# Gate of the dense experts by one ScalarE silu in place of a sigmoid and a GpSimd product

## The chip, the cores and the metric

The kernel runs on one core of a Trainium2 chip as one launch. The metric is the device time of that launch in microseconds (us). The core has these engines: TensorE (PE in the profile; its weight loads are PEld), VectorE (DVE), ScalarE (ACT), GpSimd (POOL) and SyncE (SP). Each engine carries out its own instructions in order, and semaphores hold an instruction until what it reads is written.

## The reference, cut to what matters

The whole program is a chain of eight pairs of layers on 4096 tokens of 128 features. The change lies in the sixth pair, in its first layer (named L2_attn_b in the reference, "window" in the kernel), which is an attention followed by experts of its own; it touches the experts. Every token goes through all eight experts, hence "dense"; the routing weights of four of them are not zero.

```python
def moe(x, router_W, router_b, gup, gup_b, down, down_b):
    logits = flat.astype(jnp.float32) @ router_W + router_b
    w, idx = jax.lax.top_k(logits, TOP_K)                    # TOP_K = 4 of 8
    w = jax.nn.softmax(w, axis=-1) / TOP_K
    scores = jnp.zeros((T, N_EXPERTS), w.dtype).at[jnp.arange(T)[:, None], idx].add(w)
    gate_up = jnp.einsum('th,ehm->etm', flat, gup) + gup_b[:, None, :]
    gate = jnp.clip(gate_up[..., :INTER], NEG, LIMIT)        # LIMIT = 7, INTER = 128
    up = jnp.clip(gate_up[..., INTER:], -LIMIT, LIMIT)
    glu = gate * jax.nn.sigmoid(gate * ALPHA)                # ALPHA = 1.702
    gated = (up + 1.0) * glu
    eout = jnp.einsum('etm,emh->eth', gated, down) + down_b[:, None, :]
    out = jnp.einsum('eth,te->th', eout, scores)
```

With silu(z) = z * sigmoid(z), the gate is `glu = silu(1.702 * gate) / 1.702`. Since `gated` is multiplied by the token's routing weight for the expert, the factor 1/1.702 can be put into that weight.

## The kernel before, in words

Tokens lie along the free axis: a chunk is 128 features by 512 tokens, and there are eight chunks (`NCH` = 8, `CH` = 512). `window_moe` runs 64 units of work, unit i being expert i mod 8 of chunk i div 8. `tiles_in_slots` writes the order out by hand: slot k calls each step whose turn it is, later steps of the pipeline first, and within `manual_schedule` the engines get their instructions in that order. In slot k these are `narrow(k - 4)`, `gate(k - 2)` and `wide(k)`, then, every fourth or eighth slot, the steps of routing for the following chunk, and last the steps of the next stage's norm for chunks that are done (`late`, five chunks). All instructions are recorded by helpers, so the profile gives the helpers' lines: L504 matmul, L508 transpose, L528 ACT, L531 DVE tensor by tensor, L534 POOL tensor by tensor, L538 and L540 DVE tensor by scalar, L543 DVE scalar_tensor_tensor.

- `wide(i)`: two matrix products into two PSUM banks (two PE matmuls each in the trace). DVE reads the first as `g` (bias, minimum with 7, L540), ACT takes the sigmoid of 1.702 g into `sg` (L528), DVE reads the second as `u` (bias and 1, minimum with 8, L540), and POOL multiplies `g` by `sg` into `g` (L534).
- `gate(i)`: DVE computes max(u, -6) * g (L543, `u<-u,g`); POOL multiplies by the spread routing weight `rb` (L534, `u<-u,rb`).
- `narrow(i)`: the down product (`ps<-u,w`), summed over the eight experts of a chunk in one bank. The first expert's slot starts the sum with the product of routing weights and bias (`ps<-rt,w`). POOL adds the attention's residual to `x` at the fifth expert, and DVE adds the sum to `x` at the eighth (`x<-x,ps`).
- Routing: `compare` (logits on PE; `lg`, `equal`, `ahead`, `m` on DVE, two small products on POOL, exp on ACT), `choose` (DVE: `rank`, `lg`, `m`, `wide`), `turn` (PE transposes, ACT copies to `rt`) and `shares` (PE spreads four experts' weights over 128 partitions into four banks, ACT copies them to `rb`).

PSUM is shared as three banks `ps` for `wide`, four `r` for routing, spreads and norm, and one `o` for the sum. Of `g` there are four buffers, of `u` six, of `sg` three. Exp and Ln need another ACT table than sigmoid: `logs` loads the first, and the table for sigmoid is loaded ahead of the next sigmoid by the compiler. The chunk whose sum is complete is normalised for the next stage by `ha<-ps` (ACT), `nsq` (POOL), `nrs` (Ln and Exp on ACT) and `ha<-ha,nrs` (DVE). That next stage is `mix`; four small POOL products of its weights (`Wr`, `Wk`) are placed near the end of this one.

Of the kernel before, what the change touches and what calls it, by code (L numbers as in the profile page):

```python
# [11 lines left out]
F32, BF16, I32 = mybir.dt.float32, mybir.dt.bfloat16, mybir.dt.int32  # L12
SP = mybir.EngineType.SP
AF = mybir.ActivationFunctionType
ALU = mybir.AluOpType
AX = mybir.AxisListType

P = 128
B, T, C = 16, 256, 128
NT = B * T  # L20
CH = 512
# [470 lines left out]
class Net:  # L492
# [910 lines left out]
    def window_moe(self, w, h, n1):  # L1403
        x = self.x
        with ExitStack() as st:
            p1 = self.pool(st, "e1", 1)
            rt = p1.tile([8, NT], F32, tag="rt", name="rt")
            self.route(n1, w["gate"], 4, 0.25, rt, w["gate_b"])
            p2 = self.pool(st, "e2", 2)

            ub = p1.tile([P, 16], F32, tag="ub", name="ub")
            self.ts(ub, w["gub"], 1.0, ALU.add)
            for c in range(NCH):
                s = self.chunk(c)
                po = self.bank()
                self.mm(po, w["downb"], rt[:, s], stop=False)
                for e in range(8):
                    pg, pu, pb = self.bank(), self.bank(), self.bank()
                    self.mm(pg, w["gu"][:, e * 256 : e * 256 + P], n1[:, s])
                    self.mm(pu, w["gu"][:, e * 256 + P : e * 256 + 256], n1[:, s])  # L1420
                    self.mm(pb, self.sel[:, e, :], rt[:, s])
                    g = p2.tile([P, CH], F32, tag="g", name="g")
                    u = p2.tile([P, CH], F32, tag="u", name="u")
                    sg = p2.tile([P, CH], F32, tag="sg", name="sg")
                    self.ts(g, pg, w["gub"][:, 2 * e : 2 * e + 1], ALU.add, 7.0, ALU.min)
                    self.act(sg, g, AF.Sigmoid, scale=1.702)
                    self.stt(sg, g, -1e9, sg, ALU.max, ALU.mult)
                    self.ts(u, pu, ub[:, 2 * e + 1 : 2 * e + 2], ALU.add, 8.0, ALU.min)
                    self.stt(u, u, -6.0, sg, ALU.max, ALU.mult)
                    self.tt(u, u, pb, ALU.mult)  # L1430
                    self.mm(po, w["down"][:, e * C : e * C + C], u, start=False, stop=e == 7)
                self.tt(g, h[:, s], po, ALU.add)
                self.gt(x[:, s], x[:, s], g, ALU.add)
# [216 lines left out]
class Fast(Net):  # L1650
# [896 lines left out]
    def window_moe(self, w, h, n1):  # L2547

        x, nc = self.x, self.nc
        with ExitStack() as st:  # L2550
            p = self.stage(st, "e2", 1)
            compare, choose, turn = self.route_steps(st, w["gate"], 4, 0.25, w["gate_b"], "r")

            ub = p.tile([P, 16], F32, tag="ub", name="ub")
            self.ts(ub, w["gub"], 1.0, ALU.add)
            rts, rbs, gs, us, pos = {}, {}, {}, {}, {}

            def compared(c):
                self.logs(False)
                compare(c, n1)  # L2560

            def turned(c):
                rts[c] = turn(c)

            def shares(i):
                c, half = divmod(i, 2)
                rb = p.tile([P, 4, CH], F32, tag="rb", name="rb", bufs=2)
                for r, pb in enumerate(self.four(rts[c], self.k["sel4" + "ab"[half]], "r")):
                    self.act(rb[:, r], pb, AF.Copy)
                rbs[i] = rb  # L2570

            def wide(i):
                c, e = divmod(i, 8)
                s = self.chunk(c)
                pg, pu = self.bank(), self.bank()
                self.mm(pg, w["gu"][:, e * 256 : e * 256 + P], n1[:, s])
                self.mm(pu, w["gu"][:, e * 256 + P : e * 256 + 256], n1[:, s])
                g = p.tile([P, CH], F32, tag="g", name="g", bufs=4)
                u = p.tile([P, CH], F32, tag="u", name="u", bufs=6)
                sg = p.tile([P, CH], F32, tag="sg", name="sg", bufs=3)  # L2580
                self.ts(g, pg, w["gub"][:, 2 * e : 2 * e + 1], ALU.add, 7.0, ALU.min)
                self.act(sg, g, AF.Sigmoid, scale=1.702)
                self.ts(u, pu, ub[:, 2 * e + 1 : 2 * e + 2], ALU.add, 8.0, ALU.min)

                self.gt(g, g, sg, ALU.mult)
                gs[i], us[i] = g, u

            def gate(i):
                c, e = divmod(i, 8)
                self.stt(us[i], us[i], -6.0, gs.pop(i), ALU.max, ALU.mult)  # L2590
                self.gt(us[i], us[i], rbs[i // 4][:, e % 4], ALU.mult)

            def narrow(i):
                c, e = divmod(i, 8)
                if e == 0:
                    pos[c] = self.bank("o")
                    self.mm(pos[c], w["downb"], rts[c][:8], stop=False)
                self.mm(pos[c], w["down"][:, e * C : e * C + C], us.pop(i), start=False, stop=e == 7)
                s = self.chunk(c)
                if e == 4:  # L2600
                    self.gt(x[:, s], x[:, s], h[:, s], ALU.add)
                if e == 7:
                    self.tt(x[:, s], x[:, s], pos.pop(c), ALU.add)

            with self.share(ps=3, r=4, o=1):
                many = 8 * NCH
                late = [(8 * i + at, 8, NCH - 3, f) for i, at, f in zip((1, 2, 2), (4, 1, 2), self.lead(p, "r", tables=True))]
                self.tiles_in_slots(-7, many + 4, [
                    (4, 1, many, narrow), (2, 1, many, gate), (0, 1, many, wide),
                    (-1, 4, 2 * NCH, shares), (-3, 8, NCH, turned), (-5, 8, NCH, choose), (-7, 8, NCH, compared),  # L2610
                    *late,
                ])
# [1236 lines left out]
```

## Time and profile before

| what | value |
| --- | --- |
| time of the kernel, median of three runs | 4268.84 us (4268.18 to 4270.52) |
| time of the profiled execution | 4291.23 us |
| its span, first to last instruction | 4289.4 us |
| mean granted TensorE clock over the span | 0.949 |
| PE busy in the span | 3886.8 us (91%) |
| DVE busy | 2597.7 us (61%) |
| ACT busy | 2325.8 us (54%) |
| POOL busy | 1949.6 us (45%) |
| first product of `wide`, last of `narrow` in `window_moe` | 3418.0 us, 3652.4 us after the span's start |

The times in the trace come from one profiled execution. A group of the profile is a line, an engine, an operation and what it writes and reads, with its count, its busy time and mean duration, and the idle time of its engine just before it with what ended it. The timeline shows instructions in order of their start; a bracket at the end of a line holds the idle time before it and the instruction that ended it. Matmuls are pipelined and their ends are modelled, so the busy share of PE also holds time in which it waits.

### The profile page before, as it was taken

The numbers are of one execution on the slowest core, as the hardware profiler recorded it, in microseconds if no ns is written. First come the engines' busy times: TensorE is split into PE (matmuls) and PEld (weight loads), VectorE is DVE, ScalarE is ACT, GpSimd is POOL, SyncE is SP. The second block draws the span as 40 slices with busy tenths as digits, with TensorE's granted clock in tenths as the row PEclk, the third lists the DMA queues.
The fourth block names the chain that finished last, engine by engine and source line by source line (L and its number), as shares of the span: only waits on it lengthen the run. The fifth ranks groups of instructions, "written<-read, shape, count | busy, mean of one in ns | idle before, by whom it ended". The sixth has DMA issues, their size and how long they took to land. (4 is left out here: it accounts for less than half of the span.)

```text
span 4289.4 us, 73913 instructions
## 1 busy us (share of the span) xinstructions
PE 3886.8 (91%) x28998; PEld 2214.8 (52%) x28998; DVE 2597.7 (61%) x4503; ACT 2325.8 (54%) x4741; POOL 1949.6 (45%) x1696
## 2 busy tenths in 40 slices
PE   7999999998899999984989979888999999899978
PEld 3555466465465456553965549643444343455333
DVE  4775576374577377464336633555777698386474
ACT  6665466554766466552446634444555544674432
POOL 4664365232565166315433434454555498411251
PEclk8999999988999999997999979999999999999989
DMA  1800000000000000002930039100000000000000
GB/s 60 340 1 1 11 1 2 19 1 1 20 1 2 3 1 2 1 3 96 324 112 12 17 128 319 63 19 16 1 1 1 3 1 1 15 2 18 6 0 21
DMA packets 78404, 176.43 MB, mean 41 GB/s; under 512 B 12606, under 2 KB 39108, under 8 KB 77920
## 3 DMA queue, kind: packets, MB, share of 16 engines
q1 hardware_dynamic: 65568, 148.40, 10.0%
q0 software_dynamic: 9120, 18.51, 1.2%
q8 instruction: 231, 3.78, 0.4%
q10 hardware_dynamic: 3360, 4.72, 0.3%
q14 instruction: 125, 1.02, 0.1%
HBM read 118.28 MB, written 54.20 MB: 40 GB/s over the span
## 5 line engine op out<-in xcount | busy, mean ns | idle before, releaser
L528 ACT ACTIVATE pt<-ps 128x512 f32<-128x512 f32 x640 | 339.7, 600 | 325.1 <-PE ps L504 323.7
L504 PE MATMUL ps<-hb,w 128*128 128x512 f32 (+1 forms) x960 | 466.3, 619 | 8.8 <-issue 3.3
L504 PE MATMUL ps<-w,hb 128*128 128x512 f32 (+2 forms) x896 | 406.7, 575 | 25.4 <-DVE t L531 19.5
L534 POOL TENSOR_TENSOR t<-t,t 128x512 f32<-128x512 f32 x256 | 319.3, 1269 | 161.5 <-DVE t L531 101.5
L531 DVE TENSOR_TENSOR t<-ps,tab 128x512 f32<-128x512 f32 x512 | 317.6, 681 | 85.3 <-ACT sq L528 81.8
L534 POOL TENSOR_TENSOR t<-t,ss 128x1024 f32<-128x1024 f32 x128 | 243.5, 1903 | 218.7 <-ACT ss L528 217.5
L504 PEld LDWEIGHTS ps<-hb,w 128*128 128x128 f32 (+1 forms) x960 | 179.6, 192 | 270.5 <-issue 223.6
L528 ACT ACTIVATE qkt<-ps 128x512 f32<-128x512 f32 x256 | 140.5, 595 | 309.9 <-PE ps L508 309.3
L531 DVE TENSOR_TENSOR u<-u,ps 128x384 f32<-128x384 f32 (+1 forms) x206 | 121.8, 595 | 282.9 <-PE ps L504 122.4
L531 DVE TENSOR_TENSOR ot<-ps,rd 128x512 f32<-128x512 f32 (+2 forms) x224 | 143.3, 640 | 231.8 <-ACT rd L528 231.8
L534 POOL TENSOR_TENSOR nsq<-ha 128x512 f32<-128x512 f32 x112 | 123.1, 1099 | 322.0 <-ACT ha L528 305.0
L504 PEld LDWEIGHTS ps<-w,hb 128*128 128x128 f32 x896 | 156.8, 194 | 185.1 <-issue 115.4
L534 POOL TENSOR_TENSOR both<-pt 128x1024 f32<-128x1024 f32 x64 | 151.2, 2362 | 199.9 <-DVE pt L531 164.3
L504 PE MATMUL ps<-nsq,ct 128*128 128x512 f32 x368 | 203.6, 636 | 32.5 <-POOL nsq L534 27.6
L504 PE MATMUL ps<-ot,w 128*128 128x512 f32 x448 | 214.4, 613 | 17.3 <-DVE ot L531 9.2
L504 PE MATMUL ps<-u,w 128*128 128x512 f32 (+1 forms) x448 | 218.4, 611 | 8.4 <-POOL u L534 8.4
L2199 POOL DMA_INDIRECT back<-y,x x142 | 138.9, 978 | 185.5 <-ACT y L528 84.2
L504 PE MATMUL ps<-xt,w 128*128 128x128 f32 x1704 | 219.9, 279 | 1.7 <-ACT xt L528 1.5
L528 ACT ACTIVATE u<-ps,w 128x512 f32<-128x512 f32 x160 | 107.7, 685 | 183.1 <-PE ps L504 180.5
L504 PEld LDWEIGHTS ps<-xt,w 128*128 128x128 f32 x1704 | 203.7, 193 | 3.0 <-ACT xt L528 2.6
L3746 POOL DMA_INDIRECT rows<-out,idx x128 | 126.2, 986 | 170.2 <-ACT out L528 121.1
L528 ACT ACTIVATE nrs<-ps,ct 128x512 f32<-128x512 f32 x208 | 139.6, 683 | 103.2 <-PE ps L504 93.8
(363 smaller groups left out, 9095.3 us busy)
## 6 DMA issues: line engine op xcount, KB each, us to landing
w<-in_moe_x SPq DMA_DIRECT2D x142, 533.0 KB
rows<-t SPq DMA_DIRECT2D x64, 520.0 KB
x<-rows SPq DMA_DIRECT2D x142, 65.0 KB
w<-in_local_f SPq DMA_DIRECT2D x8, 659.5 KB
y<-back ACTq DMA_DIRECT2D x16, 256.0 KB
y<-back SPq DMA_DIRECT2D x16, 256.0 KB
w<-in_local_f SPq DMA_DIRECT2D x4, 658.5 KB
back<-y,x POOLq DMA_INDIRECT x142
```

Source lines behind the costliest of these rows:

```text
L504: self.nc.tensor.matmul(out, lhsT, rhs, start=start, stop=stop)
L528: self.nc.scalar.activation(out, in_, func, **kw)
L531: self.nc.vector.tensor_tensor(out, a, b, op)
L534: self.nc.gpsimd.tensor_tensor(out, a, b, op)
L2199: nc.gpsimd.indirect_dma_start(views[i], bass.IndirectOffsetOnAxis(ap=x[:, C : C + 1].bitcast(I32), axis=0), y, None, bounds_check=2 * NT ...
L3746: nc.gpsimd.indirect_dma_start(views[(c * 2 + k) * 4 + t], bass.IndirectOffsetOnAxis(ap=idx[:, k, t : t + 1], axis=0), out[:, k, t], None,)
```

## The change

In `window_moe`, ACT computes silu(1.702 g) and writes it over `g`; the sigmoid, its tile `sg` and the POOL product of `g` and `sg` are gone. The ACT copies of the spread routing weights from PSUM to `rb` multiply by 1/1.702.

```diff
                 for r, pb in enumerate(self.four(rts[c], self.k["sel4" + "ab"[half]], "r")):
-                    self.act(rb[:, r], pb, AF.Copy)
+                    self.act(rb[:, r], pb, AF.Copy, scale=1.0 / 1.702)
                 rbs[i] = rb
...
                 u = p.tile([P, CH], F32, tag="u", name="u", bufs=6)
-                sg = p.tile([P, CH], F32, tag="sg", name="sg", bufs=3)
                 self.ts(g, pg, w["gub"][:, 2 * e : 2 * e + 1], ALU.add, 7.0, ALU.min)
-                self.act(sg, g, AF.Sigmoid, scale=1.702)
+                self.act(g, g, AF.Silu, scale=1.702)
                 self.ts(u, pu, ub[:, 2 * e + 1 : 2 * e + 2], ALU.add, 8.0, ALU.min)
-
-                self.gt(g, g, sg, ALU.mult)
                 gs[i], us[i] = g, u
```

## The prediction

> **What bounds it now.** I read first the windows view, one row for each chunk of eight experts (from the start of a second expert's first matmul to the next chunk's; the last row runs to the final expert's down product). Columns: stretch, length, then busy us (instructions) of PE, PEld, DVE, ACT, POOL, granted clock, DMA.
>
> ```profile
> 3474.28:3504.39 30.11, 29.20 (x83) 12.48 (x82) 26.65 (x38) 15.42 (x24) 27.16 (x21) 0.94 0.00 1
> 3504.39:3533.16 28.77, 27.77 (x84) 11.75 (x82) 26.39 (x38) 15.29 (x24) 25.60 (x21) 1.00 0.00 1
> 3533.16:3564.85 31.69, 30.92 (x84) 12.88 (x82) 26.08 (x38) 15.53 (x24) 27.57 (x22) 0.89 0.00 0
> 3622.90:3652.44 29.54, 23.30 (x58) 9.42 (x57) 23.06 (x25) 7.64 (x12) 28.84 (x23) 0.90 0.00 1
> ```
>
> PE, DVE and POOL are all near full; ACT is half idle. Chunks at full clock take 28.8 us, those with a clock under 1 take 29.3 to 31.7. The groups of 3450 to 3630 and the tile views (min/median/max ns) say what fills DVE and POOL:
>
> ```profile
> L534 POOL TENSOR_TENSOR g<-g,sg 128x512 f32<-128x512 f32 x50 | 75.2, 1504 | 10.9 <-ACT sg L528 10.6
> L534 POOL TENSOR_TENSOR u<-u,rb 128x512 f32<-128x512 f32 x50 | 67.5, 1350 | 6.6 <-DVE u L543 6.6
> L531 DVE TENSOR_TENSOR ahead<-lg 128x256 f32<-128x256 f32 x6 | 8.9, 1485 | 0.0
> L531 DVE TENSOR_TENSOR lg<-lg,m 128x32 f32<-128x32 f32 x6 | 5.7, 954 | 0.2
> ...
> L543 DVE SCALAR_TENSOR_TENSOR u<-u,g x64: 678/1168/1742, 3426.4 to 3647.7; 128x512 f32<-128x512 f32 x64
> ```
>
> The g product is the larger half of POOL. The DVE product takes 678 ns at best and 1168 at the median, and `lg<-lg,m`, 32 columns wide, takes 954. They are long where a POOL product runs beside them. Then the timeline at a chunk boundary (start, us, instruction, idle before and its releaser):
>
> ```profile
> 3537.09 1.49 DVE L531 TENSOR_TENSOR ahead<-lg 128x256 f32<-128x256 f32 x1
> ...
> 3538.70 1.04 DVE L531 TENSOR_TENSOR lg<-lg,m 128x32 f32<-128x32 f32 x1
> ...
> 3539.78 0.23 ACT L528 ACTIVATE lg<-lg 128x32 f32<-128x32 f32 x1 [2.56 <-DVE lg L531]
> ...
> 3542.70 0.69 DVE L531 TENSOR_TENSOR ha<-ha,nrs 128x512 f32<-128x512 f32 x1 [0.45 <-ACT nrs L528]
> ...
> 3544.05 1.97 PE L504 MATMUL ps<-rt,w 8*128 8x512 f32 x2 [0.20 <-DVE x L531]
> ```
>
> Slow routing steps on DVE delay ACT's exp, this delays the norm's Ln and Exp, `ha` and `x<-x,ps` on DVE follow, and PE waits for the last before the new chunk's bias product, as there is one bank for the sum. Half speed follows: the trace's clock records show it at 3486.2 to 3489.6, 3544.2 to 3551.0 and 3605.6 to 3609.0. Last, the tail:
>
> ```profile
> 3647.66 1.74 DVE L543 SCALAR_TENSOR_TENSOR u<-u,g 128x512 f32<-128x512 f32 x1 [2.69 <-POOL g L534]
> 3648.81 2.93 POOL L534 TENSOR_TENSOR u<-u,rb 128x512 f32<-128x512 f32 x2
> 3650.57 3.38 PE L504 MATMUL ps<-u,w 128*128 128x512 f32 x4 [4.96 <-POOL u L534]
> ```
>
> PE ends on POOL's backlog: 12.0 us lie between the last expert's first matmul (3640.46) and its down product (3652.44).
>
> **What the Trainium skill says.** "GPSIMD Engine Reference", Specifications: GpSimd's SBUF interfaces are VectorE's too, with contention for DVE instructions that have two SBUF inputs. The trace agrees: 678 ns against up to 1742 for the same product, while the PSUM-fed `g<-ps,w` stays within 737 to 752. "ScalarE: Activation LUTs", Step-by-step: one element per cycle and lane whatever the function; What ACT_TABLE_LOAD costs: about 1283 ns for any set. The trace agrees: loads take 1283, and the silu of the sparse experts (`u<-ps`, 384 columns) takes 490 ns where a copy of 512 takes 579 to 597. "TensorE: Matmul & The Clock Gate", Part 1: a gate halves the clock after a window of low activity. The trace agrees on the half (a 128x512 matmul starts every 0.43 us, in those stretches every 0.85); what triggers it no view shows.
>
> **The change, part by part.** As built, PE, DVE, ACT and SP issue the same instructions in the same order in both kernels, table loads included; POOL issues 64 products fewer. No DMA or queue moves.
>
> *ACT.* 64 sigmoids become 64 silus of the same size in the same places: nothing, covered by ACT's 13.5 idle us in each 28.8. Their exact price is unseen, as no silu from SBUF of 512 columns is in the trace: from 0.60 us (the 490 and 0.83 ns a column for 128 more) to 0.70; I take sigmoid's 0.63. The scale in 64 copies is a constant in an instruction that is there already: 0, at most the 0.1 us between a copy's fastest and slowest, hidden as well. Writing `g` in place takes away the wait for one of three `sg` buffers (1.9 us once). `g` is held, as before, until DVE's product has read it.
>
> *POOL.* Out go 64 products of 1513 ns mean in the stage, 96.8 us. The stage keeps 116 us over about 230, so POOL stops being a bound. DVE's product waits for ACT instead of POOL; behind it on DVE are the next expert's two PSUM reads, and PE waits for those, as three banks serve two per expert.
>
> *DVE.* What contends is left with half its rival. The uncontended prices: product 0.68; `equal` 0.43 and `ahead` 0.41 (their minima), `lg<-lg,m` 0.19 to 0.51, `lg<-rank,lg` 0.19 and `m` 0.17 (the first chunk, whose routing ran while POOL was idle) against 0.87 and 0.73 now. The remaining POOL product starts when DVE's own ends, and the next two DVE instructions read PSUM, so these two kinds now miss each other.
>
> *PE, steady chunks.* From the fifth expert's start (3431.77) to the 58th's (3622.90) are 191.1 us. What PE must issue there, at its full pitch: 53 slots of six matmuls at 0.429, 136.4; 13 groups of routing spreads at 1.27, 16.5; 6 bias pairs at 0.86, 5.2; 7 transposes at 0.44, 3.1; 6 router products at 0.9, 5.4; 10 pairs of the next norm at 0.86, 8.6. Sum 175.2. So 15.9 us are lost, up to 6.8 to half clock (13.65 us at half). At the boundary above PE would want the bias product at 3543.1, and DVE's `x` ended at 3544.0. Routing now needs 3.9 us (3535.87 to 3539.74); with the prices above 1.5 to 2.3, so exp, Ln, Exp, `ha` and `x` all come 1.6 to 2.4 us sooner, and PE's wait goes. What is late next: the first silu after the table loads, ready near 3543; its product stands on DVE at 3548.7, behind `x`, another product, two PSUM reads and the choice of experts, some 5 us ahead, so nothing waits. Without the waits I expect most half-clock stretches to go too; if all stay, 6.8 us stay. Taken: 12.9 of 15.9 come back (bounds: 3 and 15.9).
>
> *Head.* PE waits 1.04 us at 3427.84 for the third expert's `g`, behind routing on DVE: 0.7 (0 to 1.5).
>
> *Tail.* POOL's order is then the product of expert 61 (numbered from 0), `x` plus residual, four small products of the next stage's weights, experts 62 and 63. DVE's 61 ends near 3641.2; POOL: 1.26 + 1.27 + 1.75 + 1.26 + 1.26 from 3641.3, and PE's last down product near 3648.2 instead of 3652.4: 4.2 (2 to 6). The next stage's matmuls stand behind it on PE, so this reaches the end.
>
> Sum: 12.9 + 0.7 + 4.2 = 17.8 us of the profiled execution's 4291.2 (span 4289.4). The median of the runs, 4268.84, is 0.5% under it; scaled, 17.7. **Forecast: 4251 us.** What can be told from no change is 0.2%, 8.5 us.
>
> **Rivals.** *DVE stays the bound*: the kept product, `equal` and `ahead` on POOL still fall on DVE's routing, and the boundary moves by 0.5 us instead of 2. For: POOL's tri products start while DVE is at `ahead`. Against: the backlog on POOL that reaches into that point is gone. Then 7 boundaries give some 6 us with POOL's own relief, and the tail 4.2: 4258.5. *PE is at its limit*: PE is busy 27.2 of 28.8 us already, and the half clock belongs to the work. For: ends of matmuls are modelled, so a busy PE hides its waits. Against: in 3622.90 to 3640.46, without routing, each slot took its 2.57 us (4.68 with spreads and bias). Then only the tail counts: 4264. *Slower, by the clock*: the stages after 3655 have half-clock stretches too (the mean clock over the span is 0.949), and shifted by 18 us they may meet them at busier times. Each window of 3.41 us costs 1.7; past 11 more the gain is gone, from 16 it is slower by over 0.2%, say 4279. Against: the runs before lie within 2.3 us. A silu of over 2.3 us would make ACT the bound as well; the 490 ns speaks against it. *The change doesn't do what it says*: excluded by the built order.
>
> **Chances.** Forecast 0.70 (4246 to 4256), DVE 0.15, PE 0.11, slower 0.04. The range, 4245.5 to 4260, runs from all of the bounds regained (15.9 + 1.5 + 6) to the DVE case; it leaves out PE and slower. Faster by over 0.2% (under 4260.3): 0.84; within: 0.12; slower: 0.04.
>
> **What would show it.** Right: no `g<-g,sg` on POOL; DVE's product at a median under 0.75; `ahead` under 1 us and exp of a boundary about 2 us sooner; chunks of 27 us; clock 1.00 in most; the tail near 8 us; silu at 0.63. Wrong: chunks still at 28.8 with short DVE instructions (PE's limit), or DVE's product still over 1 us (contention with the kept product).

## The result, and the profile after

The changed kernel takes 4252.57 us (median of six runs, 4250.41 to 4255.72) against 4271.66 for the kernel before in as many runs: ratio 0.9956, 95% interval 0.9945 to 0.9968, so 19.1 us were gained. The two profiled executions differ by more (spans 4289.4 and 4249.8), because the one of before was some 20 us late already when the experts began. So I compare the stage itself, from the start of the attention's last residual sum (`ha<-ha,ps`) to the start of the last sum of experts (`x<-x,ps`): 248.1 us before (3405.88 to 3653.98), 228.6 after (3383.96 to 3612.57). The difference is 19.5 us; what follows took 1.8 us longer.

The windows view of the changed kernel: three chunks, again from a second expert's first matmul to the next chunk's, and the tail from the last expert's first matmul to the last matmul of its down product (columns as before).

```profile
3449.89:3476.92 27.03, 27.03 (x84) 12.00 (x83) 21.39 (x38) 15.54 (x24) 14.33 (x12) 1.00 0.00 1
3476.92:3503.94 27.02, 27.02 (x84) 11.99 (x82) 21.38 (x38) 15.53 (x24) 14.33 (x12) 1.00 0.00 1
3503.94:3530.96 27.02, 27.02 (x83) 11.99 (x82) 21.39 (x38) 15.53 (x24) 14.33 (x12) 1.00 0.00 0
3601.71:3611.47 9.76, 6.32 (x13) 2.45 (x11) 4.21 (x6) 1.91 (x2) 7.37 (x8) 0.80 0.00 0
```

PE is busy for the whole of each chunk, at full clock; POOL went from some 26 us a chunk to 14.3 and DVE from 26 to 21.4. The groups from 3430 to 3590 and the tile views answer to those of before:

```profile
L534 POOL TENSOR_TENSOR u<-u,rb 128x512 f32<-128x512 f32 x49 | 62.1, 1268 | 63.0 <-DVE u L543 48.5 <-ACT g L528 10.3 <-PE ps L504 4.2
L531 DVE TENSOR_TENSOR lg<-lg,m 128x32 f32<-128x32 f32 x5 | 2.5, 509 | 0.2
L531 DVE TENSOR_TENSOR ahead<-lg 128x256 f32<-128x256 f32 x5 | 2.1, 417 | 0.0
...
L543 DVE SCALAR_TENSOR_TENSOR u<-u,g x64: 678/681/1293, 3403.8 to 3605.5; 128x512 f32<-128x512 f32 x64
L528 ACT ACTIVATE g<-g x64: 629/630/632, 3399.6 to 3603.6; 128x512 f32<-128x512 f32 x64
```

The DVE product's median fell from 1168 to 681 ns, `ahead` from 1485 to 417; POOL's remaining product is no longer stretched (1268 against 1350) and POOL is idle for 12.7 of a chunk's 27.0 us. A silu takes what a sigmoid took, 630 ns at the median. The boundary, in the timeline:

```profile
3506.65 0.19 DVE L531 TENSOR_TENSOR lg<-ps,w 128x32 f32<-128x32 f32 x1
...
3507.22 0.41 DVE L531 TENSOR_TENSOR ahead<-lg 128x256 f32<-128x256 f32 x1
...
3508.31 0.23 ACT L528 ACTIVATE lg<-lg 128x32 f32<-128x32 f32 x1 [0.53 <-DVE lg L531]
...
3511.84 0.68 DVE L531 TENSOR_TENSOR x<-x,ps 128x512 f32<-128x512 f32 x1
...
3513.61 1.02 PE L504 MATMUL ps<-rt,w 8*128 8x512 f32 x2
```

The comparison, from `lg<-ps,w` to the end of `lg<-lg,m`, takes 1.62 us (3506.65 to 3508.27) where the running chunks took 3.2 to 3.9, `x` ends 1.1 us before PE starts the bias product, and PE has no wait there. The tail still has one:

```profile
3605.01 0.84 POOL L534 TENSOR_TENSOR Wr<-w 128x128 f32<-128x128 f32 x1
...
3607.44 2.48 POOL L534 TENSOR_TENSOR u<-u,rb 128x512 f32<-128x512 f32 x2
3608.75 3.78 PE L504 MATMUL ps<-u,w 128*128 128x512 f32 x4 [3.44 <-POOL u L534]
```

### The profile page after: what moved, and what is told of

Read it like the earlier page. It is cut to its first block, busy times and chain, and to the rows that moved or that the text cites. A ratio compares the mean times of both kernels' runs of the same rounds, so it can differ in the third digit from the quotient of the medians.

```text
span 4249.8 us, 73853 instructions
## 1 busy us (share of the span) xinstructions
PE 3860.8 (91%) x28998; PEld 2207.7 (52%) x28998; DVE 2557.6 (60%) x4503; ACT 2327.2 (55%) x4741; POOL 1852.0 (44%) x1632
## 5 line engine op out<-in xcount | busy, mean ns | idle before, releaser
L504 PE MATMUL ps<-w,hb 128*128 128x512 f32 (+2 forms) x896 | 403.4, 571 | 27.9 <-DVE t L531 20.9
L534 POOL TENSOR_TENSOR t<-t,t 128x512 f32<-128x512 f32 x256 | 319.3, 1268 | 160.8 <-DVE t L531 101.2
```

The source lines that it names most:

```text
L504: self.nc.tensor.matmul(out, lhsT, rhs, start=start, stop=stop)
L534: self.nc.gpsimd.tensor_tensor(out, a, b, op)
```

## The experiments

Three readings were open. *Boundary*: POOL's products slow DVE's routing, so the sum reaches `x` late and PE waits. *POOL's pace*: POOL itself set the rate. *Chain*: DVE's product had to wait for POOL's product. Ratios are to the kernel before, run beside it on the same chip; the stage is measured as above, in one execution of each kernel, and the chunk column has the second to fifth distance of two sums to `x`, in us.

| kernel | ratio (95%) | stage | chunk |
| --- | --- | --- | --- |
| before | 1 | 248.1 | 29.3 to 31.1 |
| changed | 0.9956 (0.9945 to 0.9968) | 228.6 | 27.0 to 27.1 |
| unread product, all | 1.0009 (1.0001 to 1.0017) | 253.2 | 29.0 to 31.7 |
| unread memset | 0.9969 (0.9958 to 0.9980) | 232.9 | 27.1 to 27.8 |
| unread product, first four experts | 0.9957 (0.9944 to 0.9971) | 231.1 | 27.0 to 27.3 |
| unread product, last four experts | 0.9957 (0.9944 to 0.9971) | 230.6 | 27.0 |
| unread products at the comparison | 1.0000 (0.9992 to 1.0008) | 245.6 | 28.0 to 29.8 |
| DVE delay at the comparison | 0.9980 (0.9970 to 0.9991) | 241.1 | 27.8 to 29.5 |
| before, one load fewer | 0.9994 (0.9988 to 1.0001) | 242.4 | 28.55 |
| changed, one load fewer | 0.9960 (0.9947 to 0.9973) | 228.7 | 26.7 to 27.4 |
| product on DVE | 0.9972 (0.9962 to 0.9983) | 236.7 | 27.8 to 27.9 |
| shorter tail | 0.9943 (0.9930 to 0.9957) | 225.3 | 26.7 to 27.3 |

**An unread product in the old place**, on top of the changed kernel:

```diff
+                d = p.tile([P, CH], F32, tag="d", name="d", bufs=3)
+                self.gt(d, w["gu"][:, :CH], w["gu"][:, CH : 2 * CH], ALU.mult)
                 gs[i], us[i] = g, u
```

> The changed kernel with a POOL product put back where the old one stood, 64 of 128x512, that multiplies two constant slices of the weights into a tile nobody reads. It brings back POOL's time and its clashes with DVE, but no engine waits for its result. Contention (forecast) and POOL's load as the bound: most of the gain is gone, ratio to the kernel before 0.998 to 1.001, DVE's product at a median near 1.2 us, boundary routing near 3.9 us, chunks 28 us or more. The chain (DVE had to wait for POOL's product): the gain stays, ratio 0.9955 to 0.9965, chunks 27.0 us.

Measured 1.0009: all of the gain is gone, though nobody waits for the product, and the kernel is even slightly slower than the one before. DVE's product is long again, the comparison takes 3.3 to 3.9 us, and PE waits for `x` at five boundaries (4.4 us):

```profile
L543 DVE SCALAR_TENSOR_TENSOR u<-u,g x64: 678/1158/1758, 3431.2 to 3653.0; 128x512 f32<-128x512 f32 x64
```

The chain falls: that DVE no longer waits for POOL's result is worth nothing while POOL's products stay.

**A memset of the same length** in the same place (`memset(d, 0.0)` on 128x1700).

> The changed kernel with 64 POOL memsets of 128x1700 in the same places (about 1.5 us each by the rate of the 128x2048 ones, the mean of the old product), into a tile nobody reads. It brings back POOL's time but reads no SBUF. Contention: the gain stays but for the tail, ratio 0.9955 to 0.997, DVE's product stays under 0.75 us at the median, chunks near 27.0 us. POOL's load as the bound: 27.5 us of POOL work in a chunk, so ratio 0.998 to 1.000 and chunks of 27.5 us or more.

Measured 0.9969, chunks of 27.1 but for one. A chunk in the windows view (columns as before), the groups of POOL from 3421 to 3642 (221 us), and the timeline at a comparison:

```profile
3507.74:3534.84 27.10, 27.10 (x83) 11.91 (x83) 23.72 (x39) 15.41 (x24) 27.02 (x21) 1.00 0.00 1
...
L2584 POOL MEMSET d<- 128x1700 f32 x62 | 93.8, 1512 | 0.0
L534 POOL TENSOR_TENSOR u<-u,rb 128x512 f32<-128x512 f32 x64 | 89.3, 1396 | 2.1 <-DVE u L543 2.1
...
3534.51 1.52 POOL L2584 MEMSET d<- 128x1700 f32 x1
3535.41 0.42 DVE L531 TENSOR_TENSOR ahead<-lg 128x256 f32<-128x256 f32 x1
```

POOL is busy for 27.02 of this chunk's 27.10 us (206 of the 221 us) and PE keeps its pace, so POOL's occupation alone is not the cause. The comparison took 1.31 us in most chunks: its steps keep their short times beside a memset. DVE's product did not stay short throughout (median 707 ns, mean 999). The 12 that met a memset and nothing else took 0.68 us each; the long ones all met POOL's own remaining product as well. The stage is 4.3 us longer than the changed kernel's: 1.5 ahead of the first expert, 1.0 in the tail, the rest between.

**Half of the unread products**, under `if e < 4:` and `if e >= 4:`.

> As the unread product, but only for the first four experts of each chunk (32 products), which is where DVE has the routing of the next chunk. Contention on the routing chain: over half of the loss returns, ratio 0.9975 to 0.9995, PE waits at the boundary again. POOL's load: POOL has some 21 of 27 us, so nothing returns, ratio 0.9955 to 0.9965.

> As the unread product, but only for the last four experts of each chunk (32 products), away from the routing. Contention on the routing chain: DVE's products get longer but the boundary stays fast, chunks near 27.0 us; ratio 0.9955 to 0.997, the upper end from a longer tail. POOL's load: the same as with the first four experts, 0.9955 to 0.9965. Contention on DVE's products wherever they are: ratio near 0.998.

Both measured 0.9957, the changed kernel's own gain; for the first half I had expected a loss. The trace tells why it was the wrong test: the comparison took about 1.95 us there, not 3.3 to 3.9, as the one unread product beside it stretched `equal`, ended before it, and met neither `ahead` nor `lg<-lg,m`:

```profile
3531.58 1.27 POOL L534 TENSOR_TENSOR d<-w 128x512 f32<-128x512 f32 x1
...
3532.12 1.01 DVE L531 TENSOR_TENSOR equal<-lg 128x256 f32<-128x256 f32 x1
3533.05 0.41 DVE L531 TENSOR_TENSOR ahead<-lg 128x256 f32<-128x256 f32 x1
```

What the two runs show is that 32 products with their clashes are harmless where they miss most of the comparison, although DVE's product rose to means of 864 and 980 ns against 765. With the first four experts little was left over: at five of the seven boundaries `x` ended 0.06 to 0.24 us ahead of PE's bias product, against 1.1 in the changed kernel.

**The same number of unread products, at the comparison:**

```diff
                 self.logs(False)
+                for n in range(4):
+                    d = p.tile([P, CH], F32, tag="d", name="d", bufs=4)
+                    self.gt(d, w["gu"][:, :CH], w["gu"][:, CH : 2 * CH], ALU.mult)
                 compare(c, n1)
```

> The changed kernel with four unread POOL products (128x512) just ahead of each router comparison, 32 in all, the same number as in the two half runs, but placed so that they run beside DVE's equal, ahead and lg<-lg,m. The boundary chain: the comparison takes 3.3 to 3.9 us again instead of 1.6, PE waits for x again and half clock comes back: ratio 0.9975 to 1.000. If it is the total of clashes that counts, 32 products are as harmless as in the half runs: 0.9955 to 0.9965.

Measured 1.0000. The comparison takes 3.55 us, and the timeline has the boundary of the kernel before:

```profile
3527.33 1.04 DVE L531 TENSOR_TENSOR lg<-lg,m 128x32 f32<-128x32 f32 x1
...
3532.06 0.68 DVE L531 TENSOR_TENSOR x<-x,ps 128x512 f32<-128x512 f32 x1
...
3532.79 1.12 PE L504 MATMUL ps<-rt,w 8*128 8x512 f32 x2 [0.83 <-DVE x L531]
```

Half clock is back too (3443.9 to 3450.8, 3505.4 to 3508.8). The stage lost 17.0 us against the changed kernel, but 5.8 of them lie ahead of the first expert, where the first chunk's routing stands alone and the products delay it directly; so 11.2 us are the effect on the running chunks. Products at this place cost that much, and 32 elsewhere 2.4 us of stage or less.

**A delay of DVE alone**, three unread DVE products of 128x512 in the same line (`self.tt` for `self.gt`).

> The changed kernel with three unread DVE products (128x512, 0.68 us each) just ahead of each router comparison: the comparison comes 1.9 us later, with POOL left alone. In the changed kernel the sum is added to x about 1.0 us before PE wants its bank. The boundary chain: 0.9 us and more are lost at each of seven boundaries, and half clock can follow: ratio 0.997 to 0.999, chunks of 28 us. If POOL has to be busy as well for PE to lose time: 0.9955 to 0.9965, chunks of 27.0 us.

Measured 0.998; the chunk is 27.83 us at full clock.

```profile
3516.55 1.89 DVE L531 TENSOR_TENSOR d<-w 128x512 f32<-128x512 f32 x3
...
3524.27 1.12 PE L504 MATMUL ps<-rt,w 8*128 8x512 f32 x2 [0.52 <-DVE x L531]
```

POOL does nothing more here, so a DVE that is late at the comparison is enough for PE to wait: 1.9 us of delay, less the 1.1 to spare, are the 0.8 us that the chunk grew by. The delay holds back all that follows on DVE, not the comparison alone, but PE's idle time in the running chunks is for `x` (2.6 us) but for one wait of 0.3 us for `g`. The rest of the stage's 12.4 us is half clock (3469.2 to 3472.6, 3581.8 to 3585.2, a longer stretch at the start) and 2.4 ahead of the first expert.

**One table load fewer**, in the kernel before and in the changed one: `self.lead(p, "r")` in place of `self.lead(p, "r", tables=True)`, with the table in place from the routing's exp.

> The kernel before, without the second of the two table loads for exp and Ln at the five boundaries that also carry the next norm (the table is there already from the routing's exp). Only ACT's chain from exp to the norm's factor gets 1.28 us shorter; POOL and DVE keep all their work and clashes. The boundary chain as what held PE (forecast): x is added 1.28 us sooner, PE's wait of 1.0 us goes at five boundaries and with it part of the half-clock stretches: 4 to 9 us, ratio 0.998 to 0.999, more if all half clock goes. POOL's and DVE's backlog as what held PE: they only wait a little less at one place, ratio 0.9993 to 1.0005.

> The changed kernel without the second table load at the five boundaries (the edit that was tried on the kernel before). PE issues without a gap there in the changed kernel, and the sum is added to x 1.0 us before PE wants the bank: nothing is gained, ratio 0.995 to 0.9965, chunks of 27.0 us. Were ACT's chain still on the path, up to 5 us would be gained: 0.9943 to 0.995.

In the kernel before it gave 0.9994, where the expectation had put the second reading (backlog) and not the boundary chain that it forecast; the interval holds 1. The stage in the profile was 5.7 us shorter, more than the times show. No half clock is left in its steady chunks, PE no longer waits for `x`, and the chunk still takes 28.55 us. The groups of POOL from 3450 to 3565 (115 us) and the waits there name the second limit:

```profile
L534 POOL TENSOR_TENSOR g<-g,sg 128x512 f32<-128x512 f32 x32 | 48.0, 1501 | 0.2
L534 POOL TENSOR_TENSOR u<-u,rb 128x512 f32<-128x512 f32 x33 | 47.9, 1452 | 4.4 <-PE ps L504 4.4
...
PEld ps L504 <- POOL u L534: 10.2, 8, 1.8
PE ps L504 <- POOL u L534: 3.8, 4, 1.0
```

POOL has 4.9 us idle in 115, with products stretched from 1.26 to 1.50 and 1.45 us, and PE waits for it. Without the stretch POOL's work would not fill a chunk: an estimate from the shortest durations in the trace is 16 products of 1.26 us and four others of 1.27, 1.03, 0.73 and 0.73, 24 us in all, under PE's 27.0. So two limits lay close together in the kernel before, both made by clashes of POOL and DVE: the late boundary, and POOL's pace with stretched products. From the fifth expert's start to the 58th's, PE took 175.0 us in the changed kernel, 186.5 with the products at the comparison (the late boundary, with POOL busy for 19.9 us of 28.0), 184.0 here (POOL's pace, without the late boundary) and 191.1 with both in the kernel before. The two overlap, so the gain can't be split between them by adding. In the changed kernel the same edit gave nothing (0.9960), as expected: ACT's chain is not on the path.

**The product on DVE** (sigmoid kept; `self.tt(g, g, sg, ALU.mult)` ahead of the product with `u`).

> The sigmoid and its product are kept as in the kernel before, but the product goes to DVE (just ahead of the product with u) and POOL is relieved as in the changed kernel. DVE gets 64 products of 0.68 us: 176 us busy in the changed kernel's stage plus 44 make 220 of 224. If any relief of POOL were enough: ratio 0.9955 to 0.997. If PE has to find DVE ahead of it at the boundaries: DVE becomes the bound, chunks of 28 to 30 us, ratio 0.998 to 1.003.

Measured 0.9972, between the two: POOL's relief helps, but DVE is nearly full (busy 176.5 of 180 us from 3413 to 3593), and the chunk is 27.8. So 11.4 us of the stage are gained by relieving POOL at DVE's expense, and 8.1 more by sparing DVE the product too.

**A shorter tail**, for a faster version:

```diff
-                if e == 4:
+                if e == 0:
                     self.gt(x[:, s], x[:, s], h[:, s], ALU.add)
...
-                self.gt(m[:, 0], w["W_" + n], w["mu_" + n].broadcast_to([P, P]), ALU.mult)
-                self.gt(m[:, 1], w["W_" + n], m[:, 0], ALU.subtract)
+                self.tt(m[:, 0], w["W_" + n], w["mu_" + n].broadcast_to([P, P]), ALU.mult)
+                self.tt(m[:, 1], w["W_" + n], m[:, 0], ALU.subtract)
```

> The changed kernel with a shorter tail: POOL adds the residual to x at the first expert of a chunk instead of the fifth, and the four small products of the next stage's weights go from POOL to DVE (in both mix stages). In the changed kernel POOL's last two products wait 3.7 us behind those five instructions. Expected: the last down product 3 us sooner after the last expert's start, ratio 0.9943 to 0.9953 if that reaches the end; 0.9955 or more if the next stage starts no sooner for another reason.

Measured 0.9943, the best of all. The stage is 3.3 us shorter than in the changed kernel; POOL's last products start earlier, and no half clock falls into its tail:

```profile
3605.33 2.85 POOL L534 TENSOR_TENSOR u<-u,rb 128x512 f32<-128x512 f32 x2 [1.37 <-DVE u L543]
...
3606.96 2.40 PE L504 MATMUL ps<-u,w 128*128 128x512 f32 x4 [1.52 <-POOL u L534]
```

POOL ends 1.9 us sooner after the last expert's start than in the changed kernel; the rest of the 3.3 us goes with the half clock, which is not shown to be the edit's doing. The intervals of this and of the changed kernel overlap; that the tail is shorter is shown by the trace, not by the times.

## Why the prediction was right, point by point

- *POOL stops being a bound; DVE's two-input instructions get short.* Both as said: DVE's product 681 ns (under 750 was named), the comparison 1.62 us (1.5 to 2.3).
- *`x` comes 1.6 to 2.4 us sooner, PE's wait goes.* From the comparison's start to the end of `x` were 8.1 us at the boundary shown, now 5.9: 2.25 sooner.
- *Steady chunks, 12.9 of 15.9 us back.* This term was too small. From the fifth expert's start (3409.14) to the 58th's (3584.15) are 175.0 us, against 191.1 before and the 175.2 counted for PE: all of it came back, 16.1 us, since neither a wait of PE nor half clock was left there. I had kept 3 us for stretches that would stay.
- *Head 0.7.* From the first spreads to the fifth expert: 15.8 us before, 15.1 after: 0.7.
- *Tail 4.2.* This term was too large. From the last expert's start to the last sum: 13.5 before, 10.9 after: 2.7. By the prediction's own measure, to the start of the last down product, 12.0 us became 8.9, not 7.8. The small products of the next stage took 2.4 us on POOL, not 1.75 (two of them 0.84 each beside DVE's last products, against 0.41 in the memset run), and the last down products ran at half clock (3607.6 to 3614.5), which the sum had left out. They had run so before too (3646.6 to 3653.4), a stretch that the prediction's list of half speed does not have.
- *The sum.* 16.1 + 0.7 + 2.7 = 19.5 us in the traces and 19.1 in the medians, against 17.7 forecast; that the sum came so near is in part luck, as the two errors cancel in part. The traces are one execution each, so their closeness to the medians is partly chance too.
- *Rivals.* DVE as the bound and PE at its limit of 28.8 us fall with chunks of 27.0, where PE is now at its limit. What follows the stage took 1.8 us longer, within what one execution varies: 635.5 to 637.8 us over the twelve profiles. ACT keeps its idle half: a chunk has 15.5 us of its work, as before.
- *One reading was incomplete.* The prediction put the steady loss on the boundary and on half clock after it. The kernel before with one load fewer shows that without these its chunk would still have been 28.55 us, held by POOL's stretched products. The change removes both at once, and the sum counted from PE's own work, so it was right all the same. PE's waits in the kernel before had shown both: from the fifth expert to the 58th 2.6 us for `x`, 2.2 for POOL's `u`, 1.2 for DVE's `g`. Half clock was found in the running chunks of every kernel in which PE waits for `x` at the boundary (before, unread product, at the comparison, DVE delay), once with the product on DVE, and in none of the others, even with one load fewer in the kernel before, where PE waits for POOL instead, at most 1.0 us at a time. Nor does each stretch follow a wait for `x`: those from 3462.0 (unread product) and 3443.9 (at the comparison) follow one for `g`, of 1.26 and 0.51 us. What triggers half clock was not tested by itself.

## What to carry to other kernels

Here a GpSimd product cost more than its own time: it stretched VectorE instructions with two SBUF inputs beside it (DVE's product took 1168 ns at the median, 681 after the change), and they stretched it (a mean of 1.50 us for the product that went, against 1.26 alone). Where such clashes fell decided what they cost: on the comparison, the path to a shared bank, 11.2 us, elsewhere 2.4 or less. So look at what runs beside a GpSimd product, above all at short instructions on such a path, and compare their duration with that of the same instruction while GpSimd is idle. The activation that took over the product was free here because ScalarE had 13.5 of 28.8 us idle and the constant could ride on a copy that was there already.

## What the runs showed of the hardware that was not expected

In the kernel before:

```profile
3538.25 1.44 POOL L534 TENSOR_TENSOR g<-g,sg 128x512 f32<-128x512 f32 x1
...
3622.84 1.27 POOL L534 TENSOR_TENSOR u<-u,rb 128x512 f32<-128x512 f32 x1
3622.91 1.74 DVE L543 SCALAR_TENSOR_TENSOR u<-u,g 128x512 f32<-128x512 f32 x1
3624.06 1.73 POOL L534 TENSOR_TENSOR g<-g,sg 128x512 f32<-128x512 f32 x1
```

- A small DVE instruction can be held until a POOL product ends: `lg<-lg,m` (32 columns, 0.19 us beside a memset) ran from 3538.70 to 3539.74, and the POOL product beside it, the first line above, ended at 3539.69. In all eight chunks of both kernels it ended 0.05 us after a POOL product; in seven of the changed one's this was the small `equal<-equal,ct`, so it took 0.51 us.
- A clash of large ones is nearly a queue. In the three other lines DVE's product (0.68 us alone) starts just after a POOL product, ends 0.54 us after that one's end, and the POOL product that follows takes 1.73 us instead of 1.26. From 3622.84 to 3625.79 the three take 2.95 us, where one after the other they would take 3.2.
- DVE instructions that read PSUM were not touched: `g<-ps,w` took 0.74 to 0.75 us and `x<-x,ps` 0.67 to 0.69 in both kernels.
- A POOL memset, which reads nothing, left DVE's two-input instructions alone: beside a memset only, the product took 0.68 us and `ahead` 0.42. Yet the 128x4 product with a constant that ends the choice of experts (`m<-m`, L538, one SBUF input) took up to 0.96 us beside a memset (at 3436.99), against 0.17 in the changed kernel.
